# Moving resident weight loads of a two-layer graph transformer to the places in its opening where they are used

## The chip, the cores and the metric

The kernel runs on one core of a Trainium2 chip. The metric is the device time of one execution in microseconds, as the median of several runs. Before the change it is 3093.09 us (three runs, 3091.61 to 3094.91 us). The engines are named as in the profile: PE is the matrix engine (PEld its weight loads), DVE the vector engine, ACT the scalar engine, POOL the general engine, SP the engine that does nothing here but issue DMA transfers. Each engine takes its instructions in the order in which the program wrote them.

## The reference

There are 32 graphs of 512 nodes with 256 features, and two attention layers. Both use the same integer adjacency matrix, 512 x 512 for each graph.

```python
def _layernorm(x): return (x - mean(x)) / sqrt(var(x) + 1e-5)

# layer 0: 8 heads of 32, edges made symmetric and with self loops, then an MLP
allowed = (adj > 0) | (adj.T > 0) | eye
q, k, v = split(x @ Wqkv.T + bqkv)
attn    = softmax(where(allowed, q k^T / sqrt(32), -inf))
x1      = layernorm_affine(x + (attn v) @ Wo.T + bo)
x2      = layernorm_affine(x1 + relu(x1 @ W1.T + b1) @ W2.T + b2)   # hidden width 1024
x       = _layernorm(x + x2)

# layer 1: 8 heads of 32, edges as given, no MLP
q, k, v = x @ Wq.T + bq, x @ Wk.T + bk, x @ Wv.T + bv
w       = softmax(where(adj != 0, q k^T / sqrt(32), -inf))
out     = _layernorm(x + (w v) @ Wo.T + bo)
```

The kernel works in float32.

## The kernel before

The kernel is a software pipeline over graphs. Three procedures list steps of several graphs in one fixed order: `opening` (the first three graphs start up), `period` (29 times, in the steady state) and `closing` (the last three graphs run out). Every step issues its instructions where it stands in the list, so the list is at the same time the order of PE, of ACT, of DVE, of POOL and of the DMA queue on SP.

Weights and biases stay in on-chip memory for the whole run. Building them only notes what has to be loaded, in a list:

```python
resident = []
def weight(name): ...; resident.append((w_t, w.rearrange("(c p) m -> p c m", p=P))); return w_t
def spread(name): ...      # a row of 256 values, repeated on all 128 partitions (128 KB)
def column(name): ...      # a vector laid down the partitions, as elements of 4 bytes

wqkv = weight("L0_gnn_Wqkv")
w_t, src = resident.pop()
resident.append((w_t[:, :, : 2 * D], src[:, :, : 2 * D]))        # Wqkv, columns of q and k
# ... three bias columns ...
resident.insert(3, (w_t[:, :, 2 * D :], src[:, :, 2 * D :]))     # Wqkv, columns of v
# then Wo, bo, W1, b1, W2, b2, ln1_g, ln1_b, ln2_g, ln2_b, and for layer 1
# Wq, Wk, Wv, bq, bk, bv, Wo, bo
```

The loads stand ahead of the opening, nearly all of them in a row:

```python
first, second = graphs[3:5]
first.load()                                   # x of graph 0
for dst, src in resident[:5]:                  # Wqkv in two parts, three bias columns
    nc.sync.dma_start(out=dst, in_=src)
first.cast()                                   # adjacency int32 -> bf16 in HBM (issued by POOL)
first.entries()                                # the two masks: one plain load, four transposing loads
first.again()                                  # x of graph 0 once more (as the residual)
for dst, src in resident[5:7]:                 # Wo, bo
    nc.sync.dma_start(out=dst, in_=src)
second.load(); second.again()                  # x of graph 1, twice
for dst, src in resident[7:]:                  # all the rest
    nc.sync.dma_start(out=dst, in_=src)
opening(*graphs[3:7])
for k in range(2, B - 1): period(*graphs[k + 1 : k + 6])
closing(*graphs[B : B + 3])
```

The transpose x^T of graph 0 is made by PE; for all other graphs it comes by DMA and ends on ACT:

```python
def flip(self, n, i):      # graph > 0: half of x, loaded through a transposing DMA into v  (SP)
def sort(self, n, h):      # four DMA copies v -> kT that put the 16-bit halves in order      (SP)
def join(self, n, h):      # two ACT copies kT -> xT (graph 0: four PE transposes and one ACT copy)
```

The attention steps, with the engine each instruction runs on:

```python
def scores(self, layer, k):
    s = ps_s.tile([P, HPC, N], F32, tag="s", ...)      # the pool has one buffer
    for j in range(HPC): nc.tensor.matmul(s[:, j, :], kT[...], qT[...])      # PE
    p = work.tile([P, HPC, N], F32, tag="p", ..., bufs=8)
    nc.scalar.activation(p, s, AF.Exp, scale=SCALE)                          # ACT, 128 x 2048
def masked(self, layer, k): nc.vector.tensor_tensor(p, p, mask, ALU.mult)    # DVE, 128 x 2048
def product(self, k):       # PE: p times v, summed over eight k in one bank
def pair(self, k):          # POOL: p[k] += p[k + 1] by an accumulating DMA of 1 MB
def fold(self, dst, a, b):  # DVE: p[dst] = p[a] + p[b]
def sums(self, k, hg, ...): # PE: column sums of p (the softmax denominators)
def divide(self, hg):       # DVE: multiplies by their reciprocals
def value_bias(layer):      # PE: bv @ Wo (psB), then DVE: + bo.  once(): layer 0, once1(): layer 1
def hidden(self, h, f):     # PE: W1 (psH); ACT: relu with b1
def mlp(self, i):           # PE: W2 (psF)
```

The small outputs of PE share one pool of three banks, whatever they are.

A piece of the old opening (`a` is graph 0, `b` graph 1), and the end of the old closing (`c` is the last graph):

```python
a.scores(0, 5); a.masked(0, 4); a.product(3); a.pair(2); a.masked(0, 5)
a.once1()                     # needs bv and Wo of layer 1
a.scores(0, 6)                # its exponential stands behind b.join(0, 0) on ACT
...
c.norm4(0); c.norm4(1); c.store(0, 2); c.root(4, 2, 4); c.offset(2, 4)
c.norm4(2); c.norm4(3); c.store(2, 4)          # the last graph goes out in two halves
```

Of the kernel before, what the change touches and what calls it, by code (L numbers as in the profile page):

```python
# [27 lines left out]
def kernel(ctx: ExitStack, tc: tile.TileContext, t: dict, out: bass.AP):  # L28
# [65 lines left out]
    w_t, src = resident.pop()  # L94
    resident.append((w_t[:, :, : 2 * D], src[:, :, : 2 * D]))
# [8 lines left out]
    resident.insert(3, (w_t[:, :, 2 * D :], src[:, :, 2 * D :]))  # L104
# [48 lines left out]
    def plain(pools: ExitStack):  # L153
# [26 lines left out]
        class Graph:  # L180
# [42 lines left out]
            def masks(self):  # L223

                nc.vector.tensor_tensor(self.m0, self.m0, self.m1, ALU.max)
                diagonal = self.m0.rearrange("p c (k q) -> p (c k) q", q=P)[:, :: NQ + 1, :]
                nc.vector.tensor_tensor(diagonal, diagonal, ident_b[:, None, :].to_broadcast([P, NQ, P]), ALU.max)
                nc.vector.tensor_scalar(self.m0, self.m0, 0.0, None, ALU.is_gt)
                nc.vector.tensor_scalar(self.m1, self.m1, 0.0, None, ALU.not_equal)

# [303 lines left out]
            def store(self, a=0, b=NQ):  # L534
                nc.sync.dma_start(
                    out=out[self.b].rearrange("(c p) d -> p c d", p=P)[:, a:b, :], in_=self.x2[:, a:b, :]
                )
# [170 lines left out]
        def opening(a, b, c, d):  # L708

            a.flip(0, 0)  # L710
            a.join(0, 0)
            a.join(0, 1)
            a.masks()
            a.query_key(0, 0, 0)
            a.query_key(0, 1, 0)

            a.scores(0, 0)
            a.masked(0, 0)
            a.value(0, 0)
            b.flip(0, 0)  # L720
            a.scores(0, 1)
            a.query_key(0, 1, 1)
            a.scores(0, 2)
            a.product(0)
            a.query_key(0, 0, 1)
            a.scores(0, 3)
            b.sort(0, 0)
            a.value(0, 1)
            a.scores(0, 4)
            a.masked(0, 1)  # L730
            a.masked(0, 2)
            a.masked(0, 3)
            a.product(1)
            a.product(2)
            a.pair(0)
            b.join(0, 0)
            a.scores(0, 5)
            a.masked(0, 4)
            a.product(3)
            a.pair(2)  # L740
            a.masked(0, 5)
            a.once1()
            a.scores(0, 6)
            a.sort(0, 1)
            a.once()
            a.masked(0, 6)
            b.flip(0, 1)
            a.flip(0, 1)
            b.sort(0, 1)
            a.scores(0, 7)  # L750
            a.product(4)
            a.masked(0, 7)
            b.join(0, 1)
            a.pair(4)
            b.value(0, 0)
            a.product(5)
            a.fold(2, 2, 0)
            a.fold(3, 6, 7)
            a.product(6)
            a.product(7)  # L760
            b.query_key(0, 1, 0)
            b.query_key(0, 0, 0)
            a.sums(2, 0, first=True, last=True)
            a.fold(3, 3, 4)

            b.scores(0, 0)
            b.query_key(0, 1, 1)
            a.residual()
            b.cast()
            b.residual()  # L770
            a.divide(0)
            a.sums(3, 1, first=True, last=True)
            b.scores(0, 1)
            b.query_key(0, 0, 1)
            a.divide(1)
            a.project(0, 0)
            b.scores(0, 4)
            a.project(0, 1)
            b.scores(0, 2)
            a.out0(0)  # L780
            b.value(0, 1)
            a.out0(1)
            a.root(1, 0, 2)
            c.flip(0, 0)
            b.entries()
            a.norm1(1)
            a.out0(3)
            a.norm1(0)
            a.out0(2)
            a.transpose(a.x1, 0)  # L790
            a.root(1, 2, 4)
            a.norm1(2)
            a.norm1(3)
            b.masks()
            b.scores(0, 7)
            a.hidden(0, 0)
            a.hidden(0, 6)
            a.hidden(0, 4)
            a.hidden(0, 2)
            b.scores(0, 3)  # L800
# [3 lines left out]
            b.masked(0, 0)  # L804
            b.masked(0, 7)
            b.masked(0, 3)
            a.residual1()
            c.cast()
            a.out2(0)
            b.masked(0, 4)  # L810
            a.out2(1)
            a.root(2, 0, 2)
            a.hidden(1, 0)
            b.masked(0, 1)
            b.masked(0, 2)
            a.norm2(0)
            a.hidden(1, 4)
            a.hidden(1, 6)
            a.hidden(1, 2)
            b.scores(0, 6)  # L820
# [3 lines left out]
            b.product(3)  # L824
            b.pair(0)
            b.pair(2)
            b.masked(0, 6)
            a.norm2(1)
            b.scores(0, 5)
            b.product(4)  # L830
            a.mlp(3)
            b.once1()
            b.masked(0, 5)
            a.mlp(2)
            a.out2(3)
            b.pair(4)
            a.root(3, 0, 2)
            a.root(2, 3, 4)
            a.norm3(1)
            a.norm3(0)  # L840
            a.norm2(3)
            a.transpose(a.x2, 0)
            b.once()
            a.out2(2)
            b.product(5)
            b.product(6)
            a.sort(0, 0)
            b.product(7)
            a.value(1, 0)
            a.query_key(1, 1, 0, 0)  # L850
            a.root(2, 2, 3)
            a.root(3, 3, 4)
            a.norm2(2)
            c.sort(0, 0)
            a.root(3, 2, 3)
            d.cast()
            c.flip(0, 1)
            a.norm3(3)
            a.norm3(2)
            c.sort(0, 1)  # L860
            c.entries()
            a.transpose(a.x2, 1)
            b.fold(3, 6, 7)
            c.load()
            b.fold(2, 2, 0)
            c.join(0, 0)
            a.query_key(1, 0, 0, 0)
            b.fold(3, 3, 4)
            a.query_key(1, 1, 0, 1)
            a.query_key(1, 1, 1)  # L870
            c.again()
            a.query_key(1, 0, 1)
            a.query_key(1, 0, 0, 1)
            c.join(0, 1)
            b.sums(2, 0, first=True, last=True)
            b.sums(3, 1, first=True, last=True)

            a.scores(1, 0)
            b.divide(0)
            c.query_key(0, 1, 0)  # L880
            c.query_key(0, 0, 0)
            b.divide(1)
            a.scores(1, 1)
            b.project(0, 0)
            c.value(0, 0)
            a.scores(1, 2)
            b.out0(0)
            b.out0(1)
            a.masked(1, 1)
            a.value(1, 1)  # L890
            a.masked(1, 0)
            b.project(0, 1)
            b.root(1, 0, 2)
            a.residual2()
            a.scores(1, 7)
            a.product(0)
            a.masked(1, 2)
            a.product(1)
            b.norm1(1)
            a.product(2)  # L900
            a.scores(1, 3)
            b.norm1(0)
            b.out0(3)
            b.out0(2)
            b.transpose(b.x1, 0)
            a.masked(1, 3)
            c.query_key(0, 0, 1)
            a.scores(1, 6)
            b.hidden(0, 0)
            b.root(1, 2, 4)  # L910
            a.pair(2)
            a.pair(0)
            c.masks()
            b.norm1(2)
            b.norm1(3)
            a.masked(1, 6)
            b.hidden(0, 4)
            a.scores(1, 4)
            c.value(0, 1)
            b.hidden(0, 6)  # L920
            b.hidden(0, 2)
            a.scores(1, 5)
            b.transpose(b.x1, 1)
            b.residual1()
            b.mlp(0)
            c.query_key(0, 1, 1)
            b.mlp(1)
            a.product(3)
            a.masked(1, 7)
            a.masked(1, 5)  # L930
            a.masked(1, 4)
            a.fold(2, 2, 0)
            b.out2(0)
            b.out2(1)
            a.sums(2, 0, first=True, last=True)
            b.root(2, 0, 2)
            b.norm2(0)
# [3 lines left out]
            a.product(4)  # L941
            a.product(5)
            a.product(6)
            b.norm3(0)
            b.norm3(1)
            a.pair(4)

        def closing(a, b, c):


            c.scores(0, 0)
            a.fold(3, 6, 7)
            c.masked(0, 0)
            b.hidden(1, 0)
            b.hidden(1, 2)
            c.scores(0, 7)
            b.hidden(1, 4)
            b.hidden(1, 6)
            c.scores(0, 1)
            b.mlp(3)  # L960
            a.fold(3, 3, 4)
            c.masked(0, 7)
            c.masked(0, 1)
            c.scores(0, 2)
            b.out2(3)
            a.sums(3, 1, first=True, last=True)
            a.product(7)
            a.divide(1)
            c.scores(0, 5)
            b.mlp(2)  # L970
            b.root(2, 3, 4)
            c.scores(0, 3)
            b.norm2(3)
            c.masked(0, 2)
            a.project(1, 0)
            c.product(0)
            b.out2(2)
            c.masked(0, 5)
            c.once()
            c.scores(0, 4)  # L980
            b.transpose(b.x2, 0)
            a.project(1, 1)
            c.product(1)
            a.out1(0)
            c.masked(0, 3)
            c.masked(0, 4)
            c.product(2)
            c.product(3)
            c.scores(0, 6)
            c.product(4)  # L990
            c.pair(0)
            b.root(2, 2, 3)
            c.pair(2)
            b.root(3, 3, 4)
            b.norm2(2)
            a.out1(1)
            b.root(3, 2, 3)
            a.root(4, 0, 2)
            c.pair(4)
            c.product(5)  # L1000
            b.norm3(3)
            b.norm3(2)
            a.out1(3)
            b.transpose(b.x2, 1)
            b.query_key(1, 0, 0, 0)
            a.out1(2)
# [408 lines left out]
```

## Time and profile before

| what | value |
|---|---|
| median time | 3093.09 us |
| PE busy over the span | 3052.6 us (99%) |
| DVE busy | 2648.2 us (86%) |
| ACT busy | 1706.4 us (55%) |
| POOL busy | 1039.8 us (34%) |
| DMA, moved and mean | 406.54 MB, 131 GB/s |

The span is divided by the profile into 40 slices of 77 us each. In the row for PE, the first slice has the digit 6 and the last an 8, and all the others a 9; a 9 stands for 90% or more. Where the profile lists what an instruction waited for, the name behind the arrow is the engine or the transfer that released it last. A transfer has two lengths: the time the SP engine needs to issue it, and the time from issue to landing.

### The profile page before, as it was taken

The page shows a single profiled execution, that of the slowest core. Times are in us where ns is not written, and L with a number is a line of the kernel's source. Part 1 is how long each engine was busy: PE and PEld are TensorE (multiplying, and loading weights), DVE is VectorE, ACT ScalarE, POOL GpSimd, SP SyncE. Part 2 cuts the span into 40 slices and gives each one's busy share as a digit, 9 for nine tenths or more (in the row PEclk, how much of TensorE's full clock was granted, in tenths as well). Part 3 has the DMA queues.
Part 4 walks back from the last instruction along what each step waited for, and adds up shares of the span by engine and source line. Part 5 has one row for each costly group of instructions (what it writes and reads, how often), then busy time and mean ns, then how long its engine had stood idle before and what let it go on. Part 6 is the DMA issues. An engine that isn't in the chain of part 4 may idle for free.

```text
span 3093.1 us, 44243 instructions
## 1 busy us (share of the span) xinstructions
PE 3052.6 (99%) x17218; PEld 1732.7 (56%) x17218; DVE 2648.2 (86%) x3458; ACT 1706.4 (55%) x1983; POOL 1039.8 (34%) x1254
## 2 busy tenths in 40 slices
PE   6999999999999999999999999999999999999998
PEld 2656555555555555555655555555556555555554
DVE  4798898888898888988888988889888899888887
ACT  4455655555565556655555655556555655555554
POOL 1232334332343323333333433233333334332332
PEclk8999999999999999999999999999999999999999
DMA  8776776666676666776676766668666777666542
GB/s 192 134 138 115 140 143 140 123 130 130 137 151 123 133 124 136 147 139 125 122 138 137 146 120 132 123 137 155 129 133 114 141 144 140 121 131 128 116 88 63
DMA packets 341352, 406.54 MB, mean 131 GB/s; under 512 B 149648, under 2 KB 315920, under 8 KB 316432
## 3 DMA queue, kind: packets, MB, share of 16 engines
q0 software_dynamic: 95824, 282.09, 50.8%
q1 hardware_dynamic: 245312, 121.56, 15.9%
q8 instruction: 137, 2.24, 0.3%
q14 instruction: 79, 0.65, 0.1%
HBM read 89.01 MB, written 33.55 MB: 40 GB/s over the span
## 4 chain that ended last, share of the span: by engine, by line
PE 92%; DVE 3%; DMA 2%; SPq 1%; issue 1%; ACT 1%; POOL 0%; POOLq 0%; DVEq 0%; ACTq 0%
PE psS L343 17%; PE psH L479 15%; PE psF L500 14%; PE psA L360 14%; PE psQK_None L330 10%; PE psV L313 7%; PE psO L459 7%; PE psR L400 4%; PE psQK L330 3%; PE psT L301 2%; DVE p L352 1%; DMA p<-p 1%; DMA v<-in_x_dram 1%; DMA s_L_gnn_ln_g<-in_L_gnn_ln_g_dram 0%; ACT p L347 0%
## 5 line engine op out<-in xcount | busy, mean ns | idle before, releaser
L347 ACT ACTIVATE p<-psS 128x2048 f32<-128x2048 f32 x512 | 961.8, 1879 | 652.9 <-PE psS L343 647.4
L352 DVE TENSOR_TENSOR p<-p,m 128x2048 f32<-128x2048 f32 x512 | 1155.3, 2279 | 30.3 <-ACT p L347 30.3
L434 POOL TENSOR_SCALAR rs<-mv 128x2 f32<-128x2 f32 (+1 forms) x320 | 321.7, 1005 | 935.6 <-DVE mv L429 933.6
L343 PE MATMUL psS<-qT,kT 32*128 32x512 f32 x4096 | 585.6, 641 | 8.0 <-ACT p L347 6.2
L360 PE MATMUL psA<-p,v 128*32 128x512 f32 x4096 | 491.9, 598 | 0.9 <-ACT cT L370 0.7
L500 PE MATMUL psF<-w_L_gnn_W,hT 128*128 128x256 f32 x2048 | 469.1, 383 | 0.0
L479 PE MATMUL psH<-xT,w_L_gnn_W 128*128 128x256 f32 x2048 | 467.4, 384 | 0.0
L500 PEld LDWEIGHTS psF<-w_L_gnn_W,hT 128*128 128x128 f32 x2048 | 384.5, 190 | 124.2 <-issue 77.6
L479 PEld LDWEIGHTS psH<-xT,w_L_gnn_W 128*128 128x128 f32 x2048 | 382.2, 190 | 117.5 <-issue 44.7
L379 DVE TENSOR_TENSOR p<-p,p 128x2048 f32<-128x2048 f32 x189 | 429.2, 2286 | 2.6 <-DMA p<-p 2.4
L343 PEld LDWEIGHTS psS<-qT,kT 32*128 32x128 f32 x4096 | 160.6, 184 | 305.2 <-issue 114.3
L435 POOL TENSOR_TENSOR rs<-rs,neg_half 128x2 f32<-128x2 f32 (+1 forms) x320 | 304.8, 952 | 26.8
L360 PEld LDWEIGHTS psA<-p,v 128*32 128x32 f32 x4096 | 110.2, 109 | 315.3 <-issue 233.8
L487 ACT ACTIVATE hT<-psH,c_L_gnn_b 128x256 f32<-128x256 f32 x512 | 214.8, 471 | 123.3 <-PE psH L479 119.9
L415 POOL TENSOR_TENSOR total<-total,sT 128x16 f32<-128x16 f32 x128 | 28.4, 222 | 732.7 <-DVE sT L412 732.7
L459 PE MATMUL psO<-w_L_gnn_Wo,cT 128*128 128x256 f32 x1024 | 241.2, 383 | 0.9 <-DVE cT L419 0.9
L330 PE MATMUL psQK_None<-xT,w_L_gnn_Wqkv 128*128 128x512 f32 x512 | 237.8, 598 | 2.2 <-ACT xT L289 1.6
L375 POOL DMA_DIRECT2D p<-p x189 | 186.9, 991 | 141.3 <-PE psA L360 81.0
L370 ACT COPY cT<-psA 128x512 f32<-128x512 f32 x128 | 74.9, 585 | 278.6 <-PE psA L360 278.6
L447 DVE TENSOR_TENSOR y<-psF,x 128x256 f32<-128x256 f32 x128 | 53.9, 421 | 195.9 <-PE psF L500 188.9
L459 PEld LDWEIGHTS psO<-w_L_gnn_Wo,cT 128*128 128x128 f32 x1024 | 189.5, 190 | 51.5 <-DVE cT L419 22.2
L428 DVE BATCH_NORM_STATS2 st<-y 128x6 f32<-128x256 f32 x384 | 164.3, 428 | 13.1
(68 smaller groups left out, 2938.0 us busy)
## 6 DMA issues: line engine op xcount, KB each, us to landing
p<-p POOLq DMA_DIRECT2D x189, 1024.0 KB, 7.7
x<-in_x_dram SPq DMA_DIRECT2D x64, 512.0 KB, 5.1
x<-bov POOLq DMA_DIRECT2D x64, 512.0 KB, 9.1
code<-in_adj_dram POOLq DMA_DIRECT2D x32, 512.0 KB, 6.4
m<-code SPq DMA_DIRECT2D x32, 512.0 KB, 5.6
x<-s_L_gnn_ln_b POOLq DMA_DIRECT2D x32, 512.0 KB, 10.4
x<-s_L_gnn_b POOLq DMA_DIRECT2D x32, 512.0 KB, 5.5
kT<-v SPq DMA_DIRECT2D x248, 64.0 KB, 3.4
```

The source lines that it names most:

```text
L313: nc.tensor.matmul(ps[:, j, :], self.xT[:, i, at], proj[layer][0][2][:, i, :], start=(i == 0), stop=(i == ND - 1),)
L330: nc.tensor.matmul(ps, w[:, i, c * P : (c + 1) * P], self.xT[:, i, at], start=(i == 0), stop=(i == ND - 1))
L343: nc.tensor.matmul(s[:, j, :], self.kT[at, hg, kc * P : (kc + 1) * P], self.qT[at, hg, :], start=True, stop=True)
L347: nc.scalar.activation(p, s, AF.Exp, scale=SCALE)
L352: nc.vector.tensor_tensor(p, p, m[:, k % NQ, None, :].to_broadcast([P, HPC, N]), ALU.mult)
L360: nc.tensor.matmul(self.acc[hg][j * HD : (j + 1) * HD, :], self.v[:, kc, h * HD : (h + 1) * HD], self.p[k][:, j, :], start=(kc == 0), stop ...
L379: nc.vector.tensor_tensor(self.p[dst], self.p[a], self.p[b], ALU.add)
L434: nc.gpsimd.tensor_scalar(rs, self.mv[n][:, a:b, 1:2], EPS, None, ALU.add)
L435: nc.gpsimd.tensor_tensor(rs, rs, neg_half[:, a:b, None], ALU.pow)
L459: nc.tensor.matmul(ps[:, j, :], self.cT[:, k, at], wo[layer][:, k, :], start=(k == 0), stop=(k == ND - 1))
L479: nc.tensor.matmul(ps[:, j, :], w1[:, c, at], self.xT[:, c, h * 2 * P : (h + 1) * 2 * P], start=(c == 0), stop=(c == ND - 1),)
L500: nc.tensor.matmul(ps, self.hT[h][:, f, j * P : (j + 1) * P], w2[:, f, :], start=(f == 0), stop=(f == NF - 1))
```

## The change

All loads of resident tensors become a step `constants(a, b)`, which issues the entries a to b - 1 of the list; it is called from several places of the opening. Wqkv becomes one load (entry 0). The second graph's x^T (`b.flip`) is begun right behind the first loads, ahead of the masks of the first graph. The orders of `opening` and `closing` are new as a whole; `period` stays as it was. The last graph is stored in one piece.

With the part of Wqkv gone, the entries are: 0 Wqkv, 1 to 3 its biases, 4 and 5 Wo and bo, 6 and 7 W1 and b1, 8 and 9 W2 and b2, 10 and 11 ln1, 12 and 13 ln2, 14 to 16 Wq, Wk, Wv of layer 1, 17 to 19 their biases, 20 and 21 Wo and bo of layer 1.

```diff
-    w_t, src = resident.pop()
-    resident.append((w_t[:, :, : 2 * D], src[:, :, : 2 * D]))
-    resident.insert(3, (w_t[:, :, 2 * D :], src[:, :, 2 * D :]))
+            def constants(self, a, b):
+                for dst, src in resident[a:b]:
+                    nc.sync.dma_start(out=dst, in_=src)
-            def store(self, a=0, b=NQ):        # ... [:, a:b, :]
+            def store(self):                   # the whole of it
         def opening(a, b, c, d):
+            a.load()
+            a.constants(0, 4)
             a.flip(0, 0)
+            a.constants(4, 6)
+            a.constants(17, 20)
             a.join(0, 0)
+            a.constants(10, 12)
             a.join(0, 1)
-            a.masks()
             a.query_key(0, 0, 0)
             a.query_key(0, 1, 0)
+            a.value(0, 0)
             a.scores(0, 0)
+            b.flip(0, 0)
+            a.cast()
+            a.entries()
+            a.query_key(0, 1, 1)
+            b.sort(0, 0)
+            a.scores(0, 1)
+            a.constants(20, 22)
+            a.masks()
+            a.again()
+            b.flip(0, 1)
+            b.sort(0, 1)
             ...  # a.scores 3, 2 and the masked steps
+            a.once()
+            a.product(0)
+            b.join(0, 0)
+            a.scores(0, 4); a.product(1); a.product(2); a.scores(0, 5); a.masked(0, 4)
+            a.once1()
+            a.masked(0, 5); a.product(3); a.scores(0, 6); a.pair(0)
+            a.constants(12, 14)
+            b.value(0, 0)
+            b.join(0, 1)
             ...  # the rest of a's first attention
+            a.pair(4)
+            b.query_key(0, 1, 0); b.query_key(0, 0, 0)
+            b.cast()
             ...
+            a.project(0, 1)
+            b.entries()
+            a.root(1, 0, 2)
+            a.constants(6, 8)
+            a.constants(14, 17)
+            a.constants(8, 10)
             ...
+            c.flip(0, 0); b.load(); a.root(1, 2, 4); b.again()
+            a.transpose(a.x1, 0)
             ...  # b.scores(0, 4), then a.hidden (uses W1, b1), later a.mlp (uses W2)
             ...  # a.value and a.query_key of layer 1
+            c.join(0, 0)
+            ...  # c.value(0, 0), a.scores(1, 0), two query_key, a.scores(1, 1)
+            c.join(0, 1)
         def closing(a, b, c):
             ...  # a new order of the same steps
-            c.store(0, 2)
-            c.store(2, 4)
+            c.store()
-            # the loads ahead of opening(...), as shown above, are gone
```

## The prediction

> **What bounds the kernel now.** I read the page's engine totals first, then the busy time by stretches, then what PE waited for, then the DMA queue that stands behind those waits.
>
> The totals leave little: PE is busy 3052.6 us of 3093.1, so all idle time of PE together is 40.5 us, 1.3% of the span. To see where it lies I cut the span at the places where PE stops and starts again. The columns are the stretch, its length, the busy time of PE, PEld, DVE, ACT and POOL with the number of instructions, the granted PE clock, the DMA share and GB/s.
>
> ```profile
> 0.00:34.00 34.00, 25.60 (x120) 10.49 (x120) 14.36 (x10) 15.76 (x14) 3.40 (x12) 1.00 0.88 245
> 34.00:53.30 19.30, 2.05 (x4) 1.18 (x4) 0.00 (x0) 3.26 (x4) 0.00 (x0) 0.51 0.71 174
> 53.30:64.60 11.30, 11.26 (x61) 4.50 (x61) 8.83 (x6) 5.94 (x6) 4.24 (x6) 0.77 0.38 78
> 64.60:130.00 65.40, 65.19 (x349) 40.62 (x346) 51.37 (x76) 30.32 (x39) 20.28 (x28) 1.00 0.84 133
> 130.00:141.00 11.00, 8.93 (x41) 3.70 (x41) 8.52 (x10) 5.69 (x10) 0.79 (x4) 1.00 0.63 141
> 141.00:3080.00 2939.00, 2936.33 (x16636) 1669.66 (x16634) 2558.37 (x3336) 1641.83 (x1907) 1008.34 (x1201) 1.00 0.67 130
> 3080.00:3093.10 13.10, 3.29 (x14) 2.58 (x14) 6.73 (x23) 3.64 (x7) 2.79 (x6) 0.86 0.26 85
> ```
>
> Length minus PE busy gives the idle time of each row: 8.4, 17.3, 0.0, 0.2, 2.1, 2.7 and 9.8 us. So the 2939 us in the middle lose 2.7 us, the last 13 us are a chain of normalizations behind the last product, and the one hole that an order can close is from 32 to 53 us. What ended it:
>
> ```profile
> PE psB L166 <- DMA w_L_gnn_Wo<-in_L_gnn_Wo_dram: 12.8, 1, 12.8
> PE psS L343 <- ACT p L347: 6.2, 1, 6.2
> ...
> ACT xT L289 <- DMA kT<-v: 19.9, 2, 19.3
> ```
>
> These lines come from the waits of PE and of ACT in the first 60 us (total, times, longest). The first is `once1`, which wants bv and Wo of layer 1. The second is `scores(0, 6)`, which wants its one PSUM buffer from the exponential of `scores(0, 5)`; that stood on ACT behind `b.join(0, 0)`, which waited 19.3 us for the second graph's x^T. Both waits end at the same queue, as its issues in the timeline show (start, duration):
>
> ```profile
> 17.23 0.47 SPq L1200 DMA_DIRECT2D c_L_gnn_b<-in_L_gnn_b_dram  x1
> 17.74 3.65 SPq L1200 DMA_DIRECT2D w_L_gnn_W<-in_L_gnn_W_dram  x1
> 21.43 4.20 SPq L1200 DMA_DIRECT2D s_L_gnn_b<-in_L_gnn_b_dram  x1
> ...
> 41.02 0.47 SPq L1200 DMA_DIRECT2D c_L_gnn_bv<-in_L_gnn_bv_dram  x1
> 41.53 0.47 SPq L1200 DMA_DIRECT2D w_L_gnn_Wo<-in_L_gnn_Wo_dram  x1
> 42.04 0.47 SPq L1200 DMA_DIRECT2D s_L_gnn_bo<-in_L_gnn_bo_dram  x1
> 42.55 1.27 SPq L259 DMA_TRANSPOSE v<-in_x_dram  x1
> ```
>
> An issue that normally takes 0.5 us took 3.65 and 4.20 us, and further ones were held until 40.6 us; the x^T load comes dead last, at 42.55. What stands ahead of it (W1, W2, ln1, ln2, Wq, Wk, Wv) is not used before 80 us.
>
> **What the Trainium skill says.** "DMA: Bandwidth & Descriptors", section "Anatomy of one DMA", has it that a transfer's semaphore wait is done by the issuing sequencer ahead of the dispatch, not by the DMA engines; so one waiting issue holds all behind it. The trace agrees: the first mask load is issued at 8.35 us, when the cast lands, and nothing leaves the queue between 3.8 and 8.3 us. The same page, "Rules for kernel authors", says that a last dimension that isn't contiguous becomes one descriptor per element; the trace fits it: b1, 4 KB in elements of 4 bytes, took 9.3 us to land, and the blocked issues begin right behind it. "TensorE: Matmul & The Clock Gate", section "What's actually happening", says that an idle PE falls to half its clock. The trace agrees: the clock is 0.50 from 40 to 50 us and eight score matmuls take 2.09 us at 53.34 against 1.14 later.
>
> **The change, part by part.**
>
> 1. *The hole closes.* Between 32.34 us (the end of `product(3)`) and 59.03 us (the end of `scores(0, 7)`) PE did two psB and two scores. A score is 1.07 us on the chain of waits in warm stretches; a psB is 2.05 us at half clock, so 1.0 us. Useful work is 2 x 1.07 + 2 x 1.0 = 4.1 us of 26.7, so 22.6 us are lost there: 19.0 by the two waits, the rest by the low clock and start gaps. The new order asks for bv and Wo of layer 1 and for x^T early. Counting 0.5 us an issue and 1.3 us a transposing one, SP has issued 12 loads by about 7 us, b.flip by 8, the masks (after the cast, say at 9.5) by 15, the sort by 17.5, Wo of layer 1 by 18, the second half of x^T by 20. With the 4 us from issue to landing that Wo and the transposes took, everything for `once1` is there at 22 us and b's x^T by 20 and 29. PE wants `once1` near 31 us, ACT wants the joins near 27 and 35. Gain 22.6 us.
>
> 2. *Its price at the start.* The first projection now waits for the 768 KB of Wqkv instead of 512 KB, while x and the cast also move. The old first part (issued at 1.25, 4.7 us) was there by 6.0 us, 1.4 us before its use at 7.38. Half as much again may cost up to about 1 us: I take 0.5. The masks of graph 0 have Wo, bo, ln1, half of x^T and 768 more elements of 4 bytes ahead of them, some 0.9 MB; at 245 GB/s that is 3.6 us, so they arrive at 19 to 20 instead of 15.8 us. Three us of mask making (1.23 + 0.42 + 0.69 + 0.69) follow, then 2.29 us for each masked p: ready at about 25, 28, 30 and 32 us. PE, which now fills the front with both value steps and both psB, wants these products at 26, 28, 29 and 32. Loss 1 us.
>
> 3. *The late weights.* W1 and b1 now stand behind `b.entries`, which waits for b's cast, which stands on POOL behind `pair(4)`. I count the new list of PE steps with the old timeline's lengths (score 1.1, product 1.0, value 2.0, a query/key step 1.9, half a projection 1.0 us; two scores in a row at least 3.1 us apart, for the exponential between them takes 1.88): `scores(0, 0)` then starts near 14.7 us, `once` is at 25, and `product(4)` ends near 38 us; the cast lands at 46 to 48 (7 to 9 us), four transposing issues follow, and W1 is issued at about 53 and W2 at 55. W1 took 9.6 us to land, W2 16.6 behind b1, on crowded DMA engines. From `product(4)` PE has some 24 us of steps to `hidden` (five scores 5.5, three products 3.0, a value 2.0, four query/key steps 7.6, two sums 2.0, a projection 2.0, a transpose 0.7, and about 1 of waiting), near 62 us, and with 7.2 us of `hidden`, a score and a transpose 9 us more to `mlp`. This is a near thing for W1 and b1. I take 1.5 us.
>
> 4. *The hole at 139 us.* PE lost 2.1 us in 130 to 141, 1.6 of it in one wait for ACT's join of the third graph, whose transposing load at 119.42 took 16.1 us to land. In the new order four projections' worth of PE work (a value, two query/key steps, two scores: 2.0 + 4.0 + 2.2 = 8.2 us) stands ahead of the second of these joins. Gain 2.1 us.
>
> 5. *The end.* The chain of normalizations is the same. Only the store changes: the half that was issued last took 2.3 us to land, while a whole one of 512 KB took 4.3 us. Loss 2.0 us.
>
> 6. *The rest of closing.* From 2920 to 3060 us PE idles 0.8 us, so nothing is to be had; a fold of 2.29 us moves behind the last graph's `scores(1, 0)`, where DVE has 1.85 us of slack in the old run. I count 0 with an error of 1.5 us.
>
> The steady state has the same list, and PE has 2.7 us of idle in 2939, so whatever is saved in front of it stays saved. Sum: 22.6 - 0.5 - 1.0 - 1.5 + 2.1 - 2.0 = 19.7 us, so 3093.1 - 19.7 = 3073.4 us.
>
> **The rivals.**
>
> *The DMA engines are the bound of the opening, and the hole moves.* For: the DMA share is 1.10 in 20 to 30 us and 1.02 in 30 to 40; the bytes remain, and W1, W2 and the projections of layer 1 (2.8 MB) now stand right before their use, with the residual's accumulating transfers of 15 to 19 us beside them. Against: in 50 to 60 us the DMA share is 0.22, so there is room to move them to. If it is right, PE waits 5 to 12 us at `hidden` or `mlp`, and the time is 3078 to 3085.
>
> *DVE takes over.* Without the hole, the masks and the masked products are what PE waits for. For: four masked steps of 2.29 us stand in a row from about 23 us. Against: DVE was busy 14.4 us of the first 34. That would make it 3076 to 3079.
>
> *ACT's join blocks as before*, if b's x^T comes late (the flip at 119 us took 16 us on busy engines). A delay beyond some 8 us would stop the exponentials again; 3080 to 3088.
>
> *The best case* is no wait at all: 22.6 + 2.1 with a store that costs nothing, 3068.
>
> **Range and chances.** The central case is 3073.4. Losses are more likely to be larger than to be smaller, so the range is 3067 to 3084. Faster by over 2% would need 61.9 us, more than all idle time of PE (40.5) and the low clock together: 1%. Slower by over 2% would take a new stall of 80 us: 1%. Within 2%: 98%.
>
> **What the changed profile would show.** Right: PE busy over 90% in 34 to 53 us at full clock; no wait of psB or of ACT's xT over 2 us; the end of `scores(0, 7)` near 38 us in place of 59; the hole at 139 us gone; the last store landing 4 us after its issue. PE's idle total should fall from 40.5 to about 23 us. Wrong: a PE or ACT wait for W1, b1 or W2 of over 3 us (step 3), products waiting for DVE in 20 to 35 us (step 2), or PE idle of over 3 us in the middle (then the closing's order or the phase of the steady state matters, which I hold to be free).

## The result and the profile after

| | before | after |
|---|---|---|
| median time, us | 3093.89 (3091.61 to 3094.91, 4 runs) | 3073.70 (3073.18 to 3075.26, 4 runs) |
| ratio | | 0.9937, 95% interval 0.9919 to 0.9954 |
| span of the profiled run, us | 3093.1 | 3072.4 |
| PE busy, us | 3052.6 | 3049.0 |
| PE idle, us | 40.5 | 23.4 |
| mean granted PE clock | 0.996 | 0.999 |

The changed kernel is 20 us faster, 0.63%. The prediction was 3073.4 us.

The busy time by stretches of the changed kernel, cut again where PE stops and starts (stretch, length, busy us of PE, PEld, DVE, ACT and POOL with instructions, granted PE clock, DMA share, GB/s):

```profile
0.00:34.00 34.00, 26.48 (x118) 11.60 (x119) 12.35 (x11) 17.25 (x17) 2.55 (x11) 1.00 0.75 181
34.00:53.30 19.30, 18.37 (x112) 7.30 (x114) 17.37 (x12) 12.70 (x12) 5.37 (x7) 1.00 1.02 189
53.30:64.60 11.30, 10.97 (x56) 5.55 (x48) 7.71 (x18) 6.51 (x6) 1.53 (x4) 1.00 1.22 234
64.60:110.00 45.40, 44.68 (x253) 31.29 (x254) 35.97 (x54) 18.73 (x29) 19.38 (x21) 1.00 0.94 184
110.00:121.00 11.00, 9.73 (x45) 5.05 (x48) 7.17 (x4) 6.03 (x10) 0.00 (x0) 1.00 0.93 198
121.00:3060.00 2939.00, 2936.05 (x16638) 1665.98 (x16631) 2562.13 (x3346) 1642.81 (x1907) 1007.37 (x1205) 1.00 0.67 130
3060.00:3072.40 12.40, 2.77 (x13) 2.09 (x11) 5.41 (x20) 3.27 (x6) 2.79 (x6) 0.71 0.27 90
```

The second row is the one to look at: 34 to 53 us, where PE had been busy 2.05 us at half clock, is now 18.37 of 19.30 at full clock. Idle by row is 7.5, 0.9, 0.3, 0.7, 1.3, 3.0 and 9.6 us. The DMA engines are busier there than they were: their share in the rows from 34 us on is 1.02 and 1.22, and was 0.71 and 0.38.

What PE still waits for in the first 140 us (total, times, longest):

```profile
PE psT L303 <- DMA x<-in_x_dram: 4.7, 1, 4.7
PE psQK_None L332 <- DMA w_L_gnn_Wqkv<-in_L_gnn_Wqkv_dram: 2.4, 1, 2.4
PE psS L345 <- ACT p L349: 1.3, 1, 1.3
PE psS L345 <- ACT qT L335: 0.8, 1, 0.8
PE psH L481 <- DMA w_L_gnn_W<-in_L_gnn_W_dram: 0.7, 1, 0.7
```

The waits for Wo of layer 1 and for ACT's join are gone. New are 2.4 us for Wqkv and 0.7 us for W1. The 1.3 us for an exponential belong to this wait of ACT, at 112 us:

```profile
ACT v L322 <- DMA kT<-v: 4.8, 1, 4.8
```

It is `c.value(0, 0)` copying its result into a buffer `v` out of which the third graph's `c.sort(0, 1)` was still copying x^T: both use the same tile.

Since every graph leaves through one store, the issue of the first store marks the end of the start-up. In the profiled runs, before and after:

```profile
239.71 0.42 SPq L535 DMA_DIRECT2D out_dram<-x  x1
218.69 0.42 SPq L537 DMA_DIRECT2D out_dram<-x  x1
```

So 21.0 us were gained by then, 20.7 at the end of the span. Of these 20.7 us, 17.1 are idle time of PE and 3.6 are busy time, largely matmuls that had run at half clock in and behind the hole.

### The profile page after: what moved, and what is told of

Its sections match the earlier page's. It is cut to its first block, busy times and chain, and to the rows that moved or that the text cites. A ratio compares the mean times of both kernels' runs of the same rounds, so it can differ in the third digit from the quotient of the medians.

```text
span 3072.4 us, 44237 instructions
## 1 busy us (share of the span) xinstructions
PE 3049.0 (99%) x17218; PEld 1728.9 (56%) x17218; DVE 2648.1 (86%) x3458; ACT 1707.3 (56%) x1983; POOL 1039.0 (34%) x1254
## 6 DMA issues: line engine op xcount, KB each, us to landing
x<-s_L_gnn_ln_b POOLq DMA_DIRECT2D x32, 512.0 KB, 10.4
```

## The experiments

Ratios are to the kernel before, run beside each on the same chip. "Old" orders are those of the kernel before.

| run | median us (range, runs) | ratio, 95% interval |
|---|---|---|
| Wo of layer 1 early | 3095.45 (3093.94 to 3096.88, 12) | 1.0003, 0.9995 to 1.0012 |
| x^T early | 3092.85 (3092.14 to 3093.70, 12) | 0.9995, 0.9986 to 1.0004 |
| both, bo still last | 3092.99 (3091.64 to 3096.14, 12) | 0.9997, 0.9988 to 1.0005 |
| Wo, bo and x^T early | 3082.95 (3082.10 to 3084.97, 5) | 0.9965, 0.9952 to 0.9978 |
| new orders, loads in a row | 3097.52 (3095.76 to 3110.30, 20) | 1.0014, 1.0007 to 1.0021 |
| b1 alone behind x^T | 3091.27 (3090.19 to 3093.90, 12) | 0.9994, 0.9985 to 1.0002 |
| after, Wqkv in two parts | 3073.60 (3073.13 to 3080.26, 5) | 0.9944, 0.9930 to 0.9957 |
| after, four moves | 3077.53 (3075.32 to 3079.59, 5) | 0.9946, 0.9933 to 0.9960 |
| after, W1 early | 3076.27 (3074.56 to 3079.83, 5) | 0.9945, 0.9931 to 0.9959 |
| after, value late and half stores | 3074.33 (3072.56 to 3075.63, 5) | 0.9936, 0.9922 to 0.9949 |
| after, old closing | 3073.88 (3073.01 to 3080.57, 5) | 0.9935, 0.9922 to 0.9949 |
| early loads, copies first | 3088.80 (3086.84 to 3090.22, 20) | 0.9984, 0.9977 to 0.9990 |

The intervals of the changed kernel and of its variants overlap, and each is 8 to 11 us wide. Medians of four or five runs that lie 1 to 4 us apart are not told apart by them; where such a difference is explained below, the explanation rests on the profiles.

### One of the two waits alone

Kernel before, with bv and Wo of layer 1 asked for ahead of W1 (entries of the old list: 7 W1, 8 b1, 20 bv, 21 Wo, 22 bo; bo stays last):

```diff
-            for dst, src in resident[7:]: load
+            put([20, 21]); put([7, 8, ..., 19, 22])
```

> The kernel before, with only bv and Wo of layer 1 taken out of the row of loads and issued ahead of W1; x^T of the second graph stays last. Theory (two waits lie over one another: behind the 12.8 us of once1 stands the exponential that waits for the join until 53 us, whatever once1 does): PE's wait in psB goes, but scores(0, 6) still starts near 53 us, and the time stays at 3092 to 3094 us. Rival A (the two waits add, so each can be taken away by itself): 12 us less, 3080 to 3082 us.

Kernel before, with the transposing loads of the second graph ahead of Wo, and its copies ahead of W1:

```diff
+            first.flip(0, 0); second.flip(0, 0); second.flip(0, 1)
             second.load(); second.again()
+            second.sort(0, 0); second.sort(0, 1)
             for dst, src in resident[7:]: load
```

> The kernel before, with only the second graph's x^T (two transposing loads and eight copies) issued ahead of the row of loads W1 and on; bv and Wo of layer 1 stay at the row's end, now some 6 us later. Theory (waits lie over one another): the ACT wait for the join goes, PE stands in once1 until about 48 us and goes on at once from there; 3088 to 3092 us. Rival A (the waits add): 6 us less, 3087 us, and no later once1. Rival B (x^T alone is the cause, as the few words of the change have it): 3074 to 3078 us.

Neither gained anything. The first, waits of PE in the first 60 us:

```profile
PE psS L343 <- ACT p L347: 20.8, 1, 20.8
```

The second, the same view:

```profile
PE psB L166 <- DMA w_L_gnn_Wo<-in_L_gnn_Wo_dram: 18.5, 1, 18.5
```

Before, the two waits read 12.8 and 6.2 us. With the one gone, the other reads 20.8; with the other gone, the one reads 18.5. They lay over each other, and a profile credits each moment to whichever ended it. So the sum of the two is the size of the hole, and neither line alone is the worth of its cure.

### Both, and a third wait below them

The two edits together, bo of layer 1 still at the end of the list.

> The kernel before, with both moved ahead of the row of loads, and its old orders of opening and closing, its Wqkv in two parts and its store in halves. Theory (the queue was the whole cause, and the new orders are not needed): 3070 to 3075 us, no wait of PE over 2 us between 20 and 60 us. Rival C (the gain comes from the new order of the opening, which fills PE while the loads come): 3080 us or more, with a new wait on the masks or the products.

A miss: 3092.99 us, no gain. The waits of DVE, and then those of PE in the first 140 us, of this kernel:

```profile
DVE bov L169 <- DMA s_L_gnn_bo<-in_L_gnn_bo_dram: 18.2, 1, 18.2
```

```profile
PE psA L360 <- DVE p L352: 14.7, 2, 14.4
```

`once1` adds bo on DVE, and the masked products stand behind that addition in DVE's order. In the profile of before PE stopped first, so DVE's need for bo never showed. With bo moved as well:

```diff
+            put([20, 21, 22])                 # bv, Wo and bo of layer 1
             second.load(); second.again()
             second.sort(0, 0); second.sort(0, 1)
+            put([7, 8, ..., 19])
```

> As the run with bv, Wo and x^T early in the old orders, and bo of layer 1 early as well. Theory (three waits lie over one another in the hole: PE in once1 for bv and Wo, ACT in the join for x^T, DVE in once1's sum for bo; the time falls only when the last of them goes): the 14.4 us that PE waited for DVE's masked product go, about 3 us of waiting for the join stay (the copies landed late), 3073 to 3078 us. Rival C (the new order of the opening is needed): again no gain, or under 8 us, with a fourth wait that isn't a load of a resident tensor.

3082.95 us, 10 to 11 us better than before, between what the theory and the rival gave. Behind the start, these are PE's longest waits in the first 60 us:

```profile
PE psS L343 <- ACT p L347: 3.7, 1, 3.7
PE psR L400 <- DVE p L379: 2.1, 1, 2.1
```

The first is the join again: the copies of x^T were issued from 21.8 to 29.8 us beside other loads, and the median of their landings is 9.7 us, against 2.1 in the changed kernel. The second is `sums` waiting for a `fold` of the pairs. The two profiles are 10.7 us apart, and only 4.6 of that is idle time of PE (28.0 us against 23.4); the other 6.1 is busy time (3055.1 us against 3049.0). Most of it lies behind these two waits, where the granted clock was 0.82 in 34 to 53 us and 0.86 in 53 to 65, and 1.00 in the changed kernel.

### The order alone

The changed kernel's orders of opening and closing, with all loads in a row ahead of them, as before.

```diff
-            a.load(); a.constants(0, 4); ...  # the constants called inside the opening
+            # the loads ahead of opening(...), as in the kernel before; opening without constants(...)
```

> The changed kernel with its new orders, but all resident loads in one row ahead of the opening as in the kernel before (Wqkv whole), the second graph's x^T behind them. Theory: b.join(0, 0), which now stands one exponential earlier on ACT, holds it from about 29 to 50 us, and PE with it; 3091 to 3097 us. Rival C (the order is what helps): 3074 to 3080 us.

3097.52 us, slower than before by 0.14%: the new order asks for the second graph's join earlier, and stands there longer. The profiled run was the longest of the twenty (3110.3 us), so its wait is larger than a typical one:

```profile
ACT xT L290 <- DMA kT<-v: 34.9, 2, 34.3
```

So early loads alone are worth 10 to 11 us, the order alone costs 4, and together they give 20. In these runs the order pays only where the loads come in its sequence. This is not a clean sum: the early loads stood in another place than in the changed kernel.

### What holds the queue: small elements or bytes

The prediction put the blocked issues down to b1's 4-byte elements. Kernel before, with b1's load alone moved behind the second graph's x^T:

```diff
-            for dst, src in resident[7:]: load
+            put([7, 9, 10, ..., 22])          # without b1; its load stands behind b.sort(0, 1)
```

> The kernel before, with b1 alone (4 KB as 1024 elements of 4 bytes) taken out of the row and loaded behind x^T of the second graph. Theory D (the small elements of b1 hold the queue[...]): the issues of W2 and b2 fall to about 0.5 us each, x^T is issued near 33 us instead of 42.6, and the time is 3082 to 3087 us. Rival E (the bytes of the row on full DMA engines hold it): x^T is issued at 40 to 42 us; 3091 to 3095 us.

The issues of the SP queue in this kernel (start, duration):

```profile
17.74 4.38 SPq L1192 DMA_DIRECT2D s_L_gnn_b<-in_L_gnn_b_dram  x1
...
26.35 4.46 SPq L1192 DMA_DIRECT2D w_L_gnn_Wk<-in_L_gnn_Wk_dram  x1
...
42.24 1.33 SPq L259 DMA_TRANSPOSE v<-in_x_dram  x1
```

b2, now right behind W1 and W2, is held for 4.38 us although its rows are contiguous, x^T still leaves at 42.24 us (42.55 before), and the time is the same. So b1's elements were not what held the queue. What the Trainium skill says of them ("DMA: Bandwidth & Descriptors", "Rules for kernel authors": a descriptor for each element) may well hold for b1's own landing; the prediction used it for the queue behind b1, and there it does not explain the stop. What is common to both kernels is the megabytes of W1 and W2 ahead of the stop and a DMA share over 1 while it lasts (20 to 30 and 30 to 40 us: 1.10 and 1.02 before, 1.07 and 1.05 here). That fits a queue full of bytes, but the limit itself was not measured, nor was the amount of bytes told apart from the number of pieces that they are cut into.

### The price of the whole Wqkv

The changed kernel with Wqkv's columns of q and k loaded first and those of v two loads later:

```diff
+    resident.append((w_t[:, :, : 2 * D], src[:, :, : 2 * D]))
-            a.constants(0, 4)
+            a.constants(0, 3); load(Wqkv, columns of v); a.constants(3, 4)
```

> The changed kernel with Wqkv in two parts again (q and k first, the part of v behind two bias columns). Theory (the first projection waits 2.4 us for the whole of Wqkv): it starts near 7.4 instead of 9.0 us, and the time falls by 1.7 to 2.4 us against the changed kernel, to about 3071.5 us. Rival F (the start has slack behind it, because the masks set the pace of the first products): no change, 3073 to 3074 us.

The first projection in the split kernel, in the timeline of PE (start, duration, what it waited for):

```profile
7.38 6.65 PE L335 MATMUL psQK_None<-xT,w_L_gnn_Wqkv 128*128 128x512 f32 x8 [0.68 <-ACT xT L309]
```

and in the changed kernel:

```profile
9.03 6.00 PE L332 MATMUL psQK_None<-xT,w_L_gnn_Wqkv 128*128 128x512 f32 x8 [2.36 <-DMA w_L_gnn_Wqkv<-in_L_gnn_Wqkv_dram]
```

The split starts 1.65 us earlier, needs 0.65 us more for its first eight matmuls (the last section shows why), and its first store goes out 1.15 us earlier (217.5 against 218.7 us). The medians are the same. In its profiled run 0.9 us of the lead is lost at the fourth store (last section). The rival was right on the time: the split buys nothing that can be measured. Its reason, slack behind the start, doesn't show in the profile, where 1.15 of the 1.65 us arrive at the first store.

### Four moves at once, and a collision

The changed kernel with the split, with `c.value(0, 0)` behind `c.join(0, 1)`, with W1 and b1 ahead of the second graph's masks, and with the last store in halves:

```diff
-            c.value(0, 0)                     # now behind c.join(0, 1)
+            a.constants(6, 8)                 # behind constants(12, 14); removed behind a.root(1, 0, 2)
-            c.store()
+            c.store(0, 2) ... c.store(2, 4)
```

> The changed kernel with four repairs: Wqkv in two parts, the third graph's first value step behind its second join (it waited 4.8 us on ACT for the copies of the other half, and cost PE 1.3 us), W1 and b1 ahead of the second graph's masks (PE waited 0.7 us), and the last graph stored in two halves (0.6 us more from the last normalization to the end). If each wait is worth its length: 1.7 to 2.4 + 1.3 + 0.7 + 0.6, so 4 to 5 us less than the changed kernel, about 3069 us. Rival (each wait has slack behind it): 3072 to 3074 us.

Its median is 3.8 us above the changed kernel's. The profiled run is the longest of the five. PE and the SP queue in its first 60 us:

```profile
PE psV L318 <- ACT xT L294: 4.4, 1, 4.4
```

```profile
29.35 5.34 SPq L281 DMA_DIRECT2D kT<-v  x4
```

and POOL's first accumulating transfer of 1 MB (`pair(0)`):

```profile
28.59 0.93 POOL L380 DMA_DIRECT2D p<-p  x1 [26.02 <-PE psA L365]
```

The four copies that finish the second half of x^T were issued after that megabyte. In the changed kernel they leave before it:

```profile
27.81 2.55 SPq L278 DMA_DIRECT2D kT<-v  x4
```

```profile
29.65 0.93 POOL L377 DMA_DIRECT2D p<-p  x1 [27.08 <-PE psA L362]
```

ACT waits 5.5 us for these copies, in the value's copy into `v` that stands ahead of the join. The join then comes late, PE stands for 4.4 us, and the clock falls to 0.50 for a few us behind it. Which of the four moves did it was not told apart by this run. The split was tried alone above; the next runs take W1 alone, the value step together with the half stores, and the closing.

### One move at a time

W1 and b1 ahead of the second graph's masks, nothing else:

```diff
+            a.constants(6, 8)                 # right behind a.constants(12, 14)
-            a.constants(6, 8)                 # behind a.root(1, 0, 2)
```

> The changed kernel with W1 and b1 of the first layer loaded ahead of the entries of the second graph. Theory: the hole of 0.7 us at hidden's first matmul goes, nothing else moves: 3073.0 (3072.3 to 3073.7). Rival: its 1 MB lies beside the accumulating transfers and the copies of x^T and makes them land later, as in the kernel that moved three things at once: 3074 to 3077, with a wait on the copies of x^T or on the join in the 40s.

A miss for the theory: the median is 2.6 us above the changed kernel's, and the first store 2.2 us later, though W1's 0.7 us wait is gone. Waits of PE in the first 140 us:

```profile
PE psR L402 <- DVE p L381: 2.1, 1, 2.1
PE psS L345 <- ACT p L349: 1.7, 1, 1.7
...
PE psO L461 <- DVE cT L421: 0.7, 1, 0.7
```

The first is `sums` waiting for a `fold`, which adds what the accumulating transfers of the pairs left. Their median landing in this stretch rose from 8.9 to 10.4 us, and W1 itself took 12.2 us instead of 5.9. The rival was right that W1 costs its neighbours more than it saves, but it did so through the pairs and not through x^T. A hole of 0.7 us was the cheaper place for that megabyte.

The value projection behind the join (the third graph's, `c`, and not the second's, as the expectation has it), and the half stores:

```diff
-            c.value(0, 0)                     # now behind c.join(0, 1)
-            c.store()
+            c.store(0, 2) ... c.store(2, 4)
```

> The changed kernel with the value projection of the second graph behind the join of that graph, and the last store in its two halves again. Theory: the 4.8 us wait of ScalarE at 112 us, and TensorE's 1.27 us behind it, goes, and the landing of the last half is 0.65 us shorter: 3073.7 - 1.3 - 0.6 = 3071.8 (3071 to 3072.5). Rival: the wait has slack behind it or moves to the next consumer, and the store is all that is won: 3073 to 3074.

3074.33 us: no gain to be measured. Yet its trace shows both cures working. ACT's wait of 4.8 us and PE's of 1.3 are gone; the score that stood at 119.57 us in the changed kernel,

```profile
119.57 1.14 PE L345 MATMUL psS<-qT,kT 32*128 32x512 f32 x8 [1.27 <-ACT p L349]
```

runs in this one without a wait:

```profile
116.57 1.14 PE L345 MATMUL psS<-qT,kT 32*128 32x512 f32 x8
```

(one value projection of 2 us has moved behind it). The first store is 1.07 us earlier, and the tail from ACT's last normalization to the end of the span is 3.75 us instead of 4.25. In between, 1.7 us went again in the steady state, in two places. So the theory was right on the waits, and the median shows neither.

The old closing:

```diff
-        def closing(a, b, c):  # new order
+        def closing(a, b, c):  # order of the kernel before; the whole store at the very end
```

> The changed kernel with the closing's order of the kernel before: the store as a whole at the very end, everything of the opening as changed. Theory: the new order of the closing is worth about 0.35 us (the end gained 20.7 us where the first store, ahead of the closing, had gained 21.0, and the store lost 0.65 of it), so 3073.7 within 1 us. Rival: the closing's new order is a real part of the gain and pays for what the opening did not give, then 3076 to 3079. Second rival: it costs, then 3071 to 3072.5.

3073.88 us, the same as the changed kernel: the new closing is not part of the gain. The profile happened to be of the longest of the five runs (3080.57 us), and it shows what such a run does in an unchanged opening. The SP queue and POOL:

```profile
12.51 6.36 SPq L218 DMA_TRANSPOSE m<-code  x4
18.97 2.67 SPq L278 DMA_DIRECT2D kT<-v  x4
...
29.37 5.45 SPq L278 DMA_DIRECT2D kT<-v  x4
```

```profile
29.31 0.92 POOL L377 DMA_DIRECT2D p<-p  x1 [26.76 <-PE psA L362]
```

and PE's wait:

```profile
PE psV L315 <- ACT xT L291: 3.9, 1, 3.9
```

The mask's transposing issues took 6.36 us here and 5.09 in the changed kernel's profile; everything behind them on the queue slid by that, and the second copies came 0.06 us after the megabyte instead of 1.84 us before it. Up to this point six of the profiles have almost the same program (two of them with Wqkv split):

| profile | copies issued at, for us | `pair(0)` at | PE waits for x^T | first store |
|---|---|---|---|---|
| after | 27.81, 2.55 | 29.65 | none | 218.7 |
| value late | 28.46, 3.68 | 29.76 | none | 217.6 |
| W1 early | 28.66, 3.71 | 29.09 | none | 220.9 |
| Wqkv split | 28.18, 3.57 | 28.65 | none | 217.5 |
| four moves | 29.35, 5.34 | 28.59 | 4.4 | 223.2 |
| old closing | 29.37, 5.45 | 29.31 | 3.9 | 224.6 |

Where the copies leave behind the megabyte, PE stops; where they leave ahead of it, be it by 0.5 us, it does not. So the stop of the kernel with four moves needs none of the four: this one has it with the opening unchanged, and in both the mask's issues were the longest (6.71 and 6.36 us, 5.08 to 5.57 in the other four). This is read from the order of events in six profiles. No run held the two queues apart, so whether the megabyte makes the stop or the copies were simply late is not shown. Of the 3.8 us by which the median with four moves is longer, W1 early has 2.6 by itself; how often the collision makes up the rest can't be said from one profile of each.

### Copies first, in the old order

The kernel with early Wo, bo and x^T (3082.95 us), with the copies of x^T ahead of the two loads of graph 1's x:

```diff
+            second.sort(0, 0); second.sort(0, 1)
             second.load(); second.again()
-            second.sort(0, 0); second.sort(0, 1)
```

> The kernel before with bv, Wo and bo of the first layer and the transposes of x^T ahead, in the orders of before (3082.9 us), with the second graph's copies of x^T issued ahead of its loads into the residual buffer. Theory: what kept 8 to 9 us of the gain back is that the copies of x^T land late (issues at 22 to 30 us, the join waits for them, the pair transfers fall behind): with the copies first the join's wait of 3.7 us and the stretch at a low clock behind it go, 3076 to 3079. Rival: the order of TensorE's and VectorE's work is what was missing, and it stays at 3082 to 3084.

A miss for both: 3088.80 us, 6 us slower. The join's wait did shrink, from 3.7 to 0.9 us. But the waits of PE, DVE and POOL now read:

```profile
PE psO L459 <- DVE cT L419: 11.8, 2, 10.4
```

```profile
DVE rT L418 <- POOL total L415: 12.0, 1, 12.0
```

```profile
POOL x L172 <- DMA c_L_gnn_bq<-in_L_gnn_bq_dram: 18.6, 1, 18.6
```

POOL's accumulating transfer at L172 adds ln2's beta to the residual. That beta is the fourth of the ln loads and stands in the old list behind W1, b1, W2 and b2; with the queue held (8.23 us at W2, 9.09 at b2) it was issued at 51.05 us, against 45.09 with the loads first:

```profile
51.05 0.97 SPq L1186 DMA_DIRECT2D s_L_gnn_ln_b<-in_L_gnn_ln_b_dram  x1
```

It took 7.7 us to land, and POOL, which had waited for it, went on at 59.29 us. `total`, a running sum to which the softmax denominators are added, stood behind it on POOL; `divide` writes `rT` into the buffer that `total` still had to read, so DVE stood too, and PE behind it. (The line names bq. The program and the landing name the beta, and in the kernel with the loads first the same wait, 3.9 us there, is put down to an `ln_b`.) The changed kernel asks for ln1 and ln2 before all of these, from 10 and from 30 us on. The early loads with only ln2 moved up were not run. In the kernel with the loads first POOL's wait for the beta ended at 51.7 us, 8.6 us before `total`'s turn, so there it cost PE nothing: the 9 us by which that kernel is behind the changed one come from elsewhere.

## Why the prediction was right

The time was 0.3 us off and the mechanism was the one predicted. The two largest terms were hit; the misses of the smaller ones cancel.

1. *The hole closes: right.* 22.6 us was predicted. From the end of `product(3)` to the end of `scores(0, 7)` PE needed 26.7 us before; the same work, two scores of 1.07 us and two psB of 1.06, takes 4.3 us after. That is 22.4 us. The last scores of the eight, before and after:

```profile
57.43 1.60 PE L343 MATMUL psS<-qT,kT 32*128 32x512 f32 x8
39.70 1.14 PE L345 MATMUL psS<-qT,kT 32*128 32x512 f32 x8
```

They end at 59.03 and 40.84 us, and after, one product and one value projection (2.9 us) are done in addition: 21.1 us gained, which is the 22.4 less 1.3 at the start (point 2). The queue ran later than counted (`b.flip` was issued at 10.41 us, not 8: two loads ahead of it were held for 1.65 and 2.70 us), but ACT wanted its loads later too, the joins at 29.1 and 39.3 us and not at 27 and 35. The list of what had to come early was incomplete. bo mattered as much as Wo and x^T: in the old order nothing was gained without it. And ln2's beta, counted among what is not used before 80 us, is read by POOL at 61.67 us in the profile of before.

2. *The price at the start: right in sum, wrong in its parts.* Predicted 0.5 us for Wqkv and 1.0 for the masks, together 1.5; measured 1.3 at the end of `product(3)` (35.76 us with both psB, 2.1 us, done; 32.34 before without them). Within it, the first projection starts 1.65 us later (9.03 against 7.38), and its cold group takes 6.00 us, 0.71 longer than before; that part is not Wqkv's (last section). About 1.1 us of these 2.4 come back, 0.8 of them because `value(0, 0)` now fills the gap in which PE had waited for kT. Mask making starts at 19.23 us, as predicted, but PE waits only 0.2 us for a masked product, as it had before.

3. *The late weights: right in kind, half in size.* Predicted 1.5; PE waits 0.7 us for W1. W1 was issued at 60.35 us, not 53, and the hidden layer came at 66.4, not 62. That it landed in 5.9 us, not 9.6, saved the step.

4. *The hole at 139 us: the term was mis-sized.* Gain predicted 2.1, measured 0.8 (2.07 of idle became 1.27). The join's wait is gone, but the value's copy, moved ahead of the join, waits for the same copies of x^T. Moving it behind the join took PE's idle away, which confirms the cause.

5. *The whole store: mis-sized.* Predicted a loss of 2.0; the tail from ACT's last normalization to the end is 4.25 us, 3.6 before: 0.65. The 4.3 us that I took is one landing of a whole store in the profile of before; the two stores in the closing of after took 3.0 and 3.7 us.

6. *The rest of the closing: right.* Between the first store and the tail the two profiles differ by 0.3 us in favour of the changed kernel, no more than the steady state scatters, and the old closing gives the same time.

So: +22.4 - 1.3 - 0.7 + 0.8 = 21.2, with 21.0 read at the first store; less 0.65 for the store, and 0.3 back, 20.7 in the profiled runs. Points 3 to 6 miss by +0.8, -1.3, +1.35 and +0.3 us. That they come to about 1 us, and the medians to within 0.3, is luck.

The first rival, that the DMA engines bound the opening, was wrong for this order: PE waits 0.7 us for W1, and not 5 to 12. The share over 1 from 34 us on is not free, though: with W1 moved up to 35 us the pairs landed later, and the first store was 2.2 us later. The second, that DVE takes over, was wrong: the 0.2 us of point 2 are all. The third, ACT's join blocking as before, is what happens in the two profiles in which the copies come behind the megabyte, with a stop of PE of about 4 us.

## What to carry to other kernels

Waits that lie over each other must be removed together: the profile credits the hole to the one that ended last, and two of three early loads were worth nothing while all three were worth 10 us. On a queue whose issues are held, order loads by first use on any engine, small ones too: a 128 KB bias and a beta stopped DVE and POOL, and PE behind them. Before moving a load into a stretch where the DMA engines are full, look at what the other queues issue within a few us of it.

## What was not expected

*A saved microsecond can be lost again in a steady state that is 99.9% busy.* The stores of successive graphs are 94.79 us apart, to 0.01, in most of the steady state. From the third to the fourth store the gap is 94.78 or 94.79 us in six profiles (among them before, after, W1 early and old closing) and 95.63 to 95.74 in the other eight (among them the split, the four moves and the value late). In the split and in the value late those 0.9 us are most of what they had gained; the value late lost 0.76 more between 1641 and 1737 us. The prediction said that what is saved ahead of the steady state stays saved; for gains of 1 us it did not hold in these profiles. Why the gap takes one value or the other was not looked into.

*The cold first group does not take the same time twice.* The first eight matmuls of 128x512 took 5.29 us before, 6.00 after and 6.65 in the split. The start does not set this. Before, and in the run with Wo of layer 1 early, which has the same loads ahead of it and the same start:

```profile
7.38 5.29 PE L330 MATMUL psQK_None<-xT,w_L_gnn_Wqkv 128*128 128x512 f32 x8 [0.67 <-ACT xT L304]
7.38 6.58 PE L330 MATMUL psQK_None<-xT,w_L_gnn_Wqkv 128*128 128x512 f32 x8 [0.67 <-ACT xT L304]
```

In each trace these matmuls start about 0.85 us apart at first and 0.43 us apart later. The change lies where the trace's record of the clock goes to full rate: at 10.6 us before, 13.2 with Wo early, 13.7 after, 13.4 in the split, and between 10.4 and 15.4 over all profiles. So a start that is 1.65 us earlier was worth 1.0 in the split, since more of the group ran at the slow pace. What sets the moment was not looked into.

*Half a microsecond between two queues goes with some 6 us.* With the copies 0.47 us ahead of the megabyte (the split) PE does not wait, with the copies 0.06 us behind it (the old closing) it does, and the first store is 5.9 us later than in the changed kernel, whose opening is the same. No instruction orders the two, so one program can fall on either side.
